# Graph-network kernel: 640 instead of 512 edges of a part taken from tables in SBUF, the logits of those edges turned on TensorE

## The chip, the cores and the metric

The kernel runs on one core of one Trainium2 chip. The core has five engines, each with its own in-order queue of instructions: PE (TensorE, matrix products; PEld is its weight load), DVE (VectorE), ACT (ScalarE), POOL (GpSimd, which here issues the indirect gathers) and SP (SyncE, which here only issues DMAs). The metric is device time in microseconds (us). Three runs of the kernel before gave 2940.52, 2941.33 and 2944.18 us, so the median is 2941.33 us.

## The reference

One layer of a graph network over 12,500 nodes with 128 features, and 412,500 edges that are sorted by destination (200,000 drawn edges in both directions, and a loop edge per node):

```python
theta = x[dst] - x[src]
w = sigmoid(relu(theta @ W1 + b1) @ W2 + b2)
agg = segment_sum(w * theta, dst, num_segments=n_nodes)
indeg = segment_sum(ones, dst, num_segments=n_nodes)
x = layernorm(x + agg + indeg * (x @ W4 + b4))
```

So each edge needs the row of its source, a hidden row of 128, one gate, and one weighted addition into its destination.

## The kernel before

A table z with `x @ W1` and x side by side (1 KB a node) is written to HBM first. Then the edges go by in parts. The first 18 parts ("plain") hold 1024 edges each, all of them gathered. The other edges go by in parts of `CE` = 1532. Of such a part up to 1024 edges are gathered: eight indirect DMAs on POOL (L401), each of 128 rows of z, into one of five buffers `zbuf`. The others, 512 slots, are "hot": their source is among the first 32 ranges of 256 nodes, and their rows come out of tables in SBUF (`tabs`, three bf16 terms a value) by a product with a one-hot matrix. There are 257 full hot parts and a rest of 344 edges, 258 parts in all. Two parts make a block of at most 104 destinations; a block's second part is a pass of the loop with h = 1, the first one with h = 0.

Which edge is hot is settled ahead by `place`, for 64 parts at a time: it walks the 32 ranges, and in each takes eight edges a list (a part is two lists of 766) by a MAX8 and a MATCH_REPLACE8 on DVE (L586, L589). Its steps are dealt out among the passes by a credit that each pass adds to (in `early_part` and `part`): 2.5 a pass in the hot parts before. The first such set is placed while the plain parts run, and the first hot gather needs its list of sources.

In a hot pass the engines are in an order written by hand (`manual_schedule`). PE takes, for the next part t: `hot_turned` (L1105, L1106: the hot rows' hidden values, 512 columns in the bank `pz`, first by the weights, then by the destination's row), `spread_y` (L893: the destinations' rows for the gathered edges), `hot_rows` (L1119: the logits of four groups of 128 hot edges, each a product whose moving operand is one column; L1122: the same edges' rows turned so that an edge lies on a partition), and then `issue`, which deals out the block's sums (L1158, with L1170, L1171 and L815 ahead of them where h = 1) and the 24 products of the hot tables (L1055, into the bank `pd`) in four runs. ACT takes, in this order, the relu (L1111), the sums' copy where h = 1 (L1213, L820), the hot rows' copy out of `pd` (L1069), the one-hots (L872, L873), the gates of the hot edges (L1128) and their weighing (L1131), the gates of the gathered edges (L975) and their weighing (L993), which frees the `zbuf` buffer. DVE subtracts, multiplies and adds up the gathered edges' hidden rows (L951, L956, L962), and makes the one-hots of the sums (L926, L1141), the hot tiles (L1039) and the normalization.

Of the kernel before, what the change touches and what calls it, by code (L numbers as in the profile page):

```python
# [36 lines left out]
NW = 3  # L37
AHEAD = 4
LB = 5
# [11 lines left out]
HK = HR * HS  # L51
HQ = HK // P
HOT = P * HT
LEADS = tuple(range(8))
OPENING = ((0,), (1, 7), (2, 6), (3, 5), (4,))
NU = 4
# [7 lines left out]
CE = 1532  # L64
# [5 lines left out]
HKL = HR * HE  # L70
# [14 lines left out]
def gnn_resnorm(  # L85
# [49 lines left out]
    assert HK == P * G and 2 * AW + D + WB <= 512 and LW <= SW  # L135
# [65 lines left out]
    of_buf = const.tile([P, max(HT * RG * HB * HS, BE)], F32, name="of")  # L201
    of_half = [of_buf.bitcast(BF16)[:, i * HT * RG * HB * HS:(i + 1) * HT * RG * HB * HS] for i in range(2)]
# [32 lines left out]
    wx_buf = [const.tile([P, K, AW], F32, name=f"wx{i}") for i in range(NW)]  # L235

    def table_load(c):
        n0, np_, m = chunks[c]
        xt = wx_buf[c % NW].rearrange("p k d -> p (k d)")[:, :BE]
        xt = xt.rearrange("p (t d) -> p t d", d=D)  # L240
        nc.scalar.dma_start(
            xt[:np_, :m, :], x[n0:n0 + np_ * m, :].rearrange("(p t) d -> p t d", t=m))
        return xt
# [11 lines left out]
    for name, v in (("w2_r", W2), ("b4_r", b4)):  # L255
        rows[name] = const.tile([P, D], F32, name=name)
# [13 lines left out]
    iota_row = const.tile([P, P], F32, name="iota_row")  # L270
# [36 lines left out]
    for i, t in enumerate(y2_buf):  # L307
        nc.vector.memset(t, 0.0)
        for h in range(SUB) if i < NY else (1,):
            nc.sync.dma_start(t[h * HALF + SW:h * HALF + SW + 1, :], b1.rearrange("(o d) -> o d", o=1))  # L310
# [43 lines left out]
    xT_all = const.tile([P, HX, HK], F32, name="xT")  # L354
    xT_flat = xT_all.rearrange("p j e -> p (j e)")
# [7 lines left out]
    assert late_at + 2 * NS <= HX * HK and WB + D <= 512  # L363
    hot_src = const.tile([P, NU, RG * HB * HS], F16, name="hot_src")
# [135 lines left out]
    def place(i, scratch, es, ed, bb, dp):  # L500
# [79 lines left out]
        tops = ep.tile([P, WL], F32, name="ed")[:, :HKL].rearrange("p (r e) -> p r e", e=HE)  # L580
        for r in range(HR):
# [3 lines left out]
            eight = tops[:, r, :]  # L585
            v.max(eight, left)  # L586
            v.tensor_scalar(eight, eight, FLOOR, None, op0=OP.max)
            yield "k"
            v.match_replace(left, eight, left, TAKEN)  # L589
            yield "k"  # L590
# [19 lines left out]
        yield "p"  # L610
        hrel = pp.tile([P, S2, HQ], BF16, name="hrel")
        pt = scratch()[:, :HQ * P].rearrange("p (q j) -> p q j", q=HQ)
        for q in range(HQ):
            nc.tensor.matmul(pt[:, q, :], hd[:, q * P:(q + 1) * P], ident_b, start=True, stop=True)
        yield "c"
        for q in range(HQ):
            for h in range(LISTS):
                a, e = max(h * HKL - q * P, 0), min((h + 1) * HKL - q * P, P)
                if a < e:
                    nc.scalar.activation(hrel[a:e, :, q], pt[a:e, q, h * S2:(h + 1) * S2], AF.Copy)  # L620
        hot_s = dram.tile([HR // RG, S2, LISTS, RG * HE], F16, name=f"hot_s{i}")
        rows_d = dram.tile([S2, RW], BF16, name=f"off_d{i}")
        for h, at in enumerate(lists):
            nc.sync.dma_start(hot_s[:, :n, h, :].rearrange("g p e -> p g e"),
                              hi[at].rearrange("p (g e) -> p g e", e=RG * HE))
            nc.sync.dma_start(
                rows_d[:n, BP:].rearrange("p (l m) -> p l m", l=LISTS)[:, h, :], far[at])
        hots[s0] = hot_s, hrel, n
        yield "s"
# [89 lines left out]
    with tc.manual_schedule(engines={SP}), tc.tile_pool(name="work", bufs=2) as wp, tc.tile_pool(  # L719
# [65 lines left out]
        def load_block(b):  # L785
            base = nc.values_load(base_b[0:1, b:b + 1], engines=[SP], min_val=0, max_val=N - WB,
                                  skip_runtime_bounds_check_because="base_b is at most N - WB")
            xw = wp.tile([P, D], F32, name="xw", bufs=5)
# [4 lines left out]
            if PLAIN <= b * SUB < PLAIN + NY * SUB:  # L793
                nc.vector.memset(y2[HALF:], 0.0)
            x2 = blocks[b]["x2"] = y2 if b >= W0 else x2_buf[b]
            for h in range(SUB):
# [5 lines left out]
                nc.sync.dma_start(to[h * HALF:h * HALF + SW, :], rows)  # L802
            if b * SUB >= PLAIN:
# [3 lines left out]
                for h in range(SUB):  # L807
                    nc.sync.dma_start(
                        to_all[h * HALF:(h + 1) * HALF, :],
                        rows_d[i + h:i + h + 1, :].to_broadcast([HALF, RW]))  # L810
# [71 lines left out]
        def spread_y(s):  # L882
# [3 lines left out]
            for k0 in range(0, K if s < PLAIN else J, J):  # L886
# [4 lines left out]
                d["y"].append(y)  # L891
                for j in range(J if s < PLAIN else pairs(s)):
                    nc.tensor.matmul(y[:, j, :], d["oh"][:, (k0 + j) * P:(k0 + j + 1) * P],  # L893
                                     y_of(s), start=True, stop=True)
# [73 lines left out]
        def lgh():  # L968

            return halves[1][:, :SUB * HQ].rearrange("p (i q) -> p i q", q=HQ)  # L970
# [10 lines left out]
        def weigh(s):  # L981
# [3 lines left out]
            for k in range(K):  # L985
                weighed[0] = nc.scalar.activation(wx[:, k, :D], zs[:, k, :] if s < NH else zs[:, k, D:],
                                                  AF.Copy, scale=wx[:, k, D:D + 1])

        def weigh_rest(s):

            wx = wx_of(s)
            for k in slots(s):
                weighed[0] = nc.scalar.activation(wx[:, k, :D], rows_of(s)[:, k, D:], AF.Copy,  # L993
                                                  scale=wx[:, k, D:D + 1])
# [7 lines left out]
        weighed = [None]  # L1002
# [9 lines left out]
        EP = RG * HS  # L1012
# [20 lines left out]
        def hot_tiles(f, x=0):  # L1033

            i0, g, i1, i = f
            w = (i1 - i0) * HS * RG
            of = hot_of(turn_of[0] % 2, x, w)
# [4 lines left out]
        def hot_products(f, x, pd, steps_of):  # L1042

            i0, g, i1, i = f
            w = (i1 - i0) * EP
            of = hot_of(turn_of[0] % 2, x, w)
            of = of.rearrange("p t (m r e) -> p t r m e", r=RG, e=HE)
            if not x:
                pd = ps_l.tile([P, G, P], F32, name="pd").rearrange("p g e -> p (g e)")
            bank, pd = pd, pd[:, x:x + w]  # L1050
            to = pd.rearrange("p (m r e) -> p r m e", r=RG, e=HE)
# [707 lines left out]
```

## Time and profile before

| | |
|---|---|
| median of three runs | 2941.33 us |
| the profiled execution, and its span from the first to the last instruction | 2943.8 us, 2942.0 us |
| busy share of the span: PE, PEld, DVE, ACT, POOL | 87%, 68%, 81%, 72%, 74% |
| mean granted TensorE clock | 0.937 |
| hot gathers (L401), issued from 269.3 to 2914.5 us | 2060, 980 ns each |

A row of the profile with an "x" says how many instructions it groups. A product of f32 operands stands as two records (two passes over the moving columns), so "x8" in a row of f32 products means four products. In a timeline the starts are what is added up here: a product's own duration reaches past the start of the next one.

### The profile page before, as it was taken

To read this page: it belongs to the slowest core of one execution; us is meant where nothing else is said; L and a number is where in the kernel's file an instruction comes from. 1 tells how busy PE (TensorE), PEld (TensorE's weight loads), DVE (VectorE), ACT (ScalarE), POOL (GpSimd) and SP (SyncE) were. 2 spreads that over 40 slices of the span, in tenths; PEclk is the share of its full clock that TensorE was granted. 3 is DMA by queue.
4 is the path that set the end of the run, shared out by engine and by line. 5 is a ranking of instruction groups with operands and counts; after the bars stand their busy time and mean duration, and the time that the engine had idled before them with its cause. 6 is when DMAs were issued, how large, how long until landed. Compare 5 with 4: busy or idle time off the path is not lost.

```text
span 2942.0 us, 59129 instructions
## 1 busy us (share of the span) xinstructions
PE 2548.2 (87%) x18606; PEld 2012.3 (68%) x18606; DVE 2380.3 (81%) x4436; ACT 2123.8 (72%) x6416; POOL 2164.5 (74%) x2213
## 2 busy tenths in 40 slices
PE   6877899988888998998898888898998888888886
PEld 5656677777676777776776666676776666677764
DVE  7899699888957988888558888888568888888654
ACT  6365778767777777677777777776777777677776
POOL 4566777777777777777777777777777777777774
PEclk8688999989999999999999999999999999999998
DMA  8455555555554555554554545454554555555542
GB/s 285 151 153 123 142 139 138 140 135 137 140 146 134 137 140 140 133 141 135 143 150 133 135 133 141 132 141 134 143 142 128 140 132 141 133 138 141 141 134 77
DMA packets 239329, 413.58 MB, mean 141 GB/s; under 512 B 63423, under 2 KB 147226, under 8 KB 237470
## 3 DMA queue, kind: packets, MB, share of 16 engines
q0 software_dynamic: 105280, 286.93, 35.3%
q1 hardware_dynamic: 131756, 116.40, 15.3%
q10 hardware_dynamic: 1970, 6.40, 0.7%
q8 instruction: 148, 2.42, 0.3%
q14 instruction: 175, 1.43, 0.2%
HBM read 388.57 MB, written 20.94 MB: 139 GB/s over the span
## 4 chain that ended last, share of the span: by engine, by line
PE 38%; ACT 19%; DVE 15%; DMA 11%; issue 7%; POOL 1%; DVEq 0%; SPq 0%; ACTq 0%; POOLq 0%
PE pa L1158 14%; DMA zbuf<-z,src_i 10%; DVE zbuf L951 5%; PE y L893 5%; PE pd L1055 5%; ACT wx L993 5%; PE px L1119 4%; ACT wxh L1131 4%; PE pz L1105 3%; PE pz L1106 3%; PE pz L1122 3%; ACT oh L872 2%; ACT oh L873 2%; ACT xT L1069 1%; ACT a L1213 1%
## 5 line engine op out<-in xcount | busy, mean ns | idle before, releaser
L401 POOL DMA_INDIRECT zbuf<-z,src_i x2060 | 2018.5, 980 | 637.0 <-issue 236.6
L993 ACT ACTIVATE wx<-zbuf,wx 128x128 f32<-128x128 f32 x2060 | 630.2, 388 | 0.0
L1158 PE MATMUL pa<-wx,ow 128*104 128x260 f32 (+1 forms) x2284 | 628.4, 393 | 0.0
L893 PEld LDWEIGHTS y<-y,oh 128*128 128x128 f32 (+1 forms) x2156 | 276.1, 197 | 420.5 <-DVE zbuf L951 378.2
L1055 PEld LDWEIGHTS <-tabs 128*128 128x128 bf16 x6360 | 452.8, 101 | 124.2 <-issue 8.2
L951 DVE TENSOR_TENSOR zbuf<-y,zbuf 128x1024 f32<-128x1024 f32 x258 | 315.1, 1221 | 272.2 <-DMA zbuf<-z,src_i 270.9
L1055 PE MATMUL pd<-of,tabs 128*128 128x128 bf16 (+3 forms) x6360 | 535.2, 223 | 0.0
L1111 ACT ACTIVATE hr<-pz 128x512 f32<-128x512 f32 x258 | 152.9, 593 | 522.9 <-PE pz L1106 522.8
L893 PE MATMUL y<-y,oh 128*128 128x128 f32 (+1 forms) x2156 | 314.7, 291 | 228.7 <-DVE zbuf L951 220.6
L1158 PEld LDWEIGHTS pa<-wx,ow 128*104 128x104 f32 x2284 | 342.8, 179 | 40.6 <-issue 0.4
L962 DVE TENSOR_REDUCE lg<-zbuf 128x8 f32<-128x1024 f32 x273 | 329.8, 1208 | 13.2
L956 DVE SCALAR_TENSOR_TENSOR zbuf<-zbuf,fix 128x1024 f32<-128x1024 f32 x273 | 331.6, 1215 | 9.3
L1158 PE MATMUL pa<-wxh,owh 128*104 128x130 f32 x2064 | 329.0, 296 | 0.0
L1131 ACT ACTIVATE wxh<-pz,wxh 128x128 f32<-128x128 f32 x1032 | 295.2, 369 | 42.1 <-PE pz L1122 35.9
L1105 PE MATMUL pz<-xT,wni 128*128 128x512 f32 x516 | 278.5, 621 | 1.6 <-ACT wxh L1131 1.6
L1158 PEld LDWEIGHTS pa<-wxh,owh 128*104 128x104 f32 x2064 | 274.3, 186 | 0.0
L1119 PEld LDWEIGHTS px<-w_c,hr 128*128 128x128 f32 x2064 | 263.5, 200 | 7.8 <-ACT hr L1111 7.8
L1119 PE MATMUL px<-w_c,hr 128*128 128x1 f32 x2064 | 262.1, 248 | 5.6 <-ACT hr L1111 5.6
L1106 PE MATMUL pz<-oh,y 128*128 128x512 f32 x516 | 264.5, 594 | 0.1
L872 ACT ACTIVATE oh<-to_all,away,mine 128x512 f32<-128x512 bf16 (+1 forms) x257 | 213.6, 831 | 3.1 <-DMA to_all<-off_d 3.1
L1106 PEld LDWEIGHTS pz<-oh,y 128*128 128x128 f32 x516 | 98.2, 191 | 124.3 <-issue 123.4
L1122 PE MATMUL pz<-wni,xT 128*128 128x128 f32 x1032 | 176.3, 297 | 0.0
(304 smaller groups left out, 3595.8 us busy)
## 6 DMA issues: line engine op xcount, KB each, us to landing
to_all<-off_d SPq DMA_DIRECT2D x258, 128.0 KB
zbuf<-z,src_i POOLq DMA_INDIRECT x2060
hot_src<-hot_s SPq DMA_DIRECT2D x228, 128.0 KB
y<-z SPq DMA_DIRECT2D x270, 28.0 KB
xw<-in_x_dram SPq DMA_DIRECT2D x138, 52.0 KB
out_dram<-o SPq DMA_DIRECT2D x138, 52.0 KB
wx<-in_x_dram ACTq DMA_DIRECT2D x12, 512.0 KB
z<-zbuf SPq DMA_DIRECT2D x6, 1024.0 KB
```

Of the source, the lines that this page charges most:

```text
L401: ins = nc.gpsimd.indirect_dma_start(out=rows_of(s)[:, k, :], out_offset=None, in_=z if s >= NH else x, in_offset=IndirectOffsetOnAxis(ap= ...
L893: nc.tensor.matmul(y[:, j, :], d["oh"][:, (k0 + j) * P:(k0 + j + 1) * P], y_of(s), start=True, stop=True)
L951: nc.vector.tensor_sub(half, yy.to_broadcast([P, 2, n, D]), half)
L956: nc.vector.scalar_tensor_tensor(h[:, at, :], h[:, at, :], 0.0, w2.to_broadcast([P, n, D]), op0=OP.max, op1=OP.mult)
L962: nc.vector.tensor_reduce(lg[:, at, 0], h[:, at, :], AX.X, OP.add)
L993: weighed[0] = nc.scalar.activation(wx[:, k, :D], rows_of(s)[:, k, D:], AF.Copy, scale=wx[:, k, D:D + 1])
L1055: steps_of.append(lambda q=q, i=i, t=t, j=j: nc.tensor.matmul(to[:, q], tabs[:, g, i, q, t, :], of[:, t, q], start=j == 0, stop=j == HT * ...
L1105: nc.tensor.matmul(pz, wneg, xT, start=True, stop=False)
L1106: nc.tensor.matmul(pz, y_of(t), blocks[t // SUB]["oh"][:, BP:], start=False, stop=True)
L1119: nc.tensor.matmul(lgh()[:, t % SUB, q:q + 1], hr[:, at], w2_c, start=True, stop=True)
L1131: nc.scalar.activation(wx[:, q, :D], pz[:, q * P:(q + 1) * P], AF.Copy, scale=wx[:, q, D:D + 1])
L1158: return [lambda i=i, one=one, w=w: nc.tensor.matmul(to if len(w.shape) == 3 else to[:, 0, :], one, w, start=first and i == 0, stop=last a ...
```

## The change

A part has 1608 edges of which 640 slots are hot: in each group of four ranges the first one gives 16 edges a list, the other three give 8 (`RU` = 5 units for `RG` = 4 ranges). That makes 245 full hot parts and a rest of 108 edges, 246 parts in place of 258, and four sets for `place` in place of five. What is done for 640 hot edges no longer fits one bank of 512: `hot_turned` and the relu are split in two lists of 320 (`pz` and `halves[1]`), the destination's rows of the two lists are taken from two halves of the partitions (64 each), `hot_rows` makes the logits as rows (five products with 32 equal columns of `W2`, each for 128 edges), the sigmoid runs on these rows (`hot_gates`), and PE turns the gates so that an edge is on a partition (`hot_gates_turned`), ahead of the sums and products. `hot_out` comes behind the gates. The products of the tables stay 24 for a part, six of them with 256 columns in place of 128. Loads differ too: each destination row goes to both halves, and `to_all` comes in four DMAs a block in place of two. The credit is 2.8 a pass and 6.5 in a plain part (5.5 before). Some buffers have fewer copies.

```diff
-NW = 3
+NW = 2
-LB = 5
+LB = 4
+RU = RG + 1
+HK = HR // RG * RU * HS
+ST = 32
-NU = 4
+NU = 3
-CE = 1532
+CE = 1608
...
         for r in range(HR):
...
-            eight = tops[:, r, :]
-            v.max(eight, left)
-            v.tensor_scalar(eight, eight, FLOOR, None, op0=OP.max)
-            yield "k"
-            v.match_replace(left, eight, left, TAKEN)
-            yield "k"
+            for _ in range(1 if r % RG else 2):
+                eight = tops[:, u, :]
+                u += 1
+                v.max(eight, left)
+                v.tensor_scalar(eight, eight, FLOOR, None, op0=OP.max)
+                yield "k"
+                v.match_replace(left, eight, left, TAKEN)
+                yield "k"
...
+                oh, rows = d["oh"], y_of(s)
+                if s >= PLAIN:
+                    at = slice(s % SUB * HALF, (s % SUB + 1) * HALF)
+                    oh, rows = oh[at], rows[at]
...
         def hot_turned(t):
...
-            nc.tensor.matmul(pz, wneg, xT, start=True, stop=False)
-            nc.tensor.matmul(pz, y_of(t), blocks[t // SUB]["oh"][:, BP:], start=False, stop=True)
+            oh = blocks[t // SUB]["oh"][:, BP + t % SUB * HKL:][:, :HKL]
+            banks = pz[:, :HKL], halves[1][:, :HKL]
+            for l, to in enumerate(banks):
+                nc.tensor.matmul(to, wneg, xT[:, l * HKL:(l + 1) * HKL], start=True, stop=False)
+            for l, to in enumerate(banks):
+                at = slice(l * HALF, (l + 1) * HALF)
+                nc.tensor.matmul(to, y_of(t)[at], oh[at], start=False, stop=True)
...
-            nc.scalar.activation(hr, pz, AF.Relu)
+            for l, bank in enumerate((pz, halves[1])):
+                nc.scalar.activation(hr[:, l * HKL:(l + 1) * HKL], bank[:, :HKL], AF.Relu)
...
-                nc.tensor.matmul(lgh()[:, t % SUB, q:q + 1], hr[:, at], w2_c, start=True, stop=True)
+                nc.tensor.matmul(rowed(q), w2_c.to_broadcast([P, ST]), hr[:, at], start=True, stop=True)
...
+        def hot_gates(t):
+
+            nc.scalar.activation(parts[t]["hr"][:, :2 * P], pz[:, 2 * P:], AF.Sigmoid, bias=b2_c)
+
+        def hot_gates_turned(t):
+
+            gates = parts[t]["hr"]
+            nc.tensor.transpose(pz[:, 2 * P:3 * P], gates[:, :P], ident)
+            for q in range(G, HQ):
+                at = slice((q - G) * ST, (q - G + 1) * ST)
+                newest[0] = nc.tensor.transpose(pz[:, 2 * P + q * ST:2 * P + (q + 1) * ST],
+                                                gates[at, P:2 * P], ident[at, at])
...
-            credit[0] = min(credit[0] + 2.5, 5.0)
+            credit[0] = min(credit[0] + 2.8, 5.0)
...
             if t < NS:
                 hot_rows(t)
+            if t < NS:
+                hot_gates(t)
+                hot_gates_turned(t)
+            while opened:
+                hot_out(*opened.pop(0))
+            last_out()
...
-                if h == 0:
+                if h == 1:
                     one_hot_h(b)
```

Two places of the order of instructions show it. On PE, in a pass with h = 0, from the start of `hot_turned` to the first products of the tables. Before (`px` is the bank of the logits, `pa` that of the sums, `owh` and `wxh` the hot edges' one-hots and weighed rows):

```order
L1105 MATMUL pz<-xT,wni 128x512
L1106 MATMUL pz<-oh,y_148 128x512
L893 MATMUL y<-y_146,oh 128x128 x4
L1119 MATMUL px<-w_c,hr 128x1 x4
L1122 MATMUL pz<-wni,xT 128x128 x4
L1158 MATMUL pa<-a,sh 104x130
L1158 MATMUL pa<-wxh,owh 104x130 x2
L1055 LDWEIGHTS tabs
L1055 MATMUL pd<-of,tabs 128x16x8
```

After (here `px` is the second bank, `halves[1]`; L1135 and L1138 are `hot_turned`, L910 `spread_y`, L1152 and L1155 `hot_rows`, L1164 and L1167 the gates' turn, L1203 the sums, L1081 the tables' products):

```order
L1135 MATMUL pz<-xT,wni 128x320
L1135 MATMUL px<-xT,wni 128x320
L1138 MATMUL pz<-oh,y_147 128x320
L1138 MATMUL px<-oh,y_147 128x320
L910 MATMUL y<-y_142,oh 128x128 x4
L1152 MATMUL pz<-hr,w_c 32x128 x5
L1155 MATMUL pz<-wni,xT 128x128 x2
L1155 MATMUL px<-wni,xT 128x128 x3
L1164 MATMUL pz<-wni,hr 128x128
L1167 MATMUL pz<-wni,hr 128x32
L1203 MATMUL pa<-a,sh 104x130
L1203 MATMUL pa<-wxh,owh 104x130 x2
```

Two products of 512 columns became four of 320, the products of one column became five of 128 columns on 32 output partitions, and two turns stand ahead of the sums. On ACT, in the same kind of pass, from the relu to the weighing of the hot edges, before:

```order
L1111 ACTIVATE hr<-pz 128x512
L1069 ACTIVATE xT<-pd 128x14x32
L1069 ACTIVATE xT<-pd 128x2x32
L872 ACTIVATE oh<-to_all,away,mine 128x512
L873 ACTIVATE oh<-oh 128x512
L1128 ACTIVATE wxh<-px,b_c 128x4
L1131 ACTIVATE wxh<-pz,wxh 128x128 x4
```

After:

```order
L1144 ACTIVATE hr<-pz 128x320
L1144 ACTIVATE hr<-px 128x320
L1159 ACTIVATE hr<-pz,b_c 128x256
L1096 ACTIVATE xT<-pd 128x14x32
L1096 ACTIVATE xT<-pd 128x2x32
L1096 ACTIVATE xT<-px 128x14x8
L1096 ACTIVATE xT<-px 128x2x8
L885 ACTIVATE oh<-to_all,away,mine 128x640
L886 ACTIVATE oh<-oh 128x640
L1174 ACTIVATE wxh<-pz 128x5
L1177 ACTIVATE wxh<-pz,wxh 128x128 x2
L1177 ACTIVATE wxh<-px,wxh 128x128 x3
```

The sigmoid (L1159) moved up to right behind the relu, so ACT now waits there for PE's logits, and five activations more stand in the pass.

186 lines of the change are left out of this document (107 added, 79 removed).

## The prediction

> **What bounds the kernel now.** I read the waits first, then the row of the gathers, then one long stretch by windows, and only then PE's timeline.
>
> ```profile
> POOL zbuf L401 <- issue: 260.0, 853, 0.3
> ACT hr L1111 <- PE pz L1106: 522.8, 196, 5.6
> PEld y L893 <- DVE zbuf L951: 378.2, 197, 9.7
> DVE zbuf L951 <- DMA zbuf<-z,src_i: 270.9, 138, 6.5
> ```
>
> ```profile
> L401 POOL DMA_INDIRECT zbuf<-z,src_i x2060: 942/949/1957, 269.3 to 2914.5; - x188
> ```
>
> ```profile
> 300.00:2700.00 2400.00, 2125.04 (x15778) 1675.80 (x15778) 1981.79 (x3591) 1783.97 (x5501) 1831.45 (x1866) 0.95 0.51 138
> ```
>
> ACT waits for PE, PE for DVE, DVE for the gathers' data, and POOL for nothing: its longest wait ahead of a hot gather is 0.3 us, the gap that always stands between two of them. From 269.3 to 2914.5 us it issues 2060 gathers, one in 1.2847 us. So the busiest engine by share, PE with 87%, is not the bound; the gathers' pace on POOL is. A block of two parts (16 gathers) takes 20.5 us, and 129 such pairs fill the 2645 us. The 269 us ahead and 27 us behind the last gather are opening and end.
>
> How much room PE has under that pace stands in a pair in which it did not wait:
>
> ```profile
> 1518.08 1.08 PE L1105 MATMUL pz<-xT,wni 128*128 128x512 f32 x2
> 1518.99 1.02 PE L1106 MATMUL pz<-oh,y 128*128 128x512 f32 x2
> 1519.85 1.05 PE L893 MATMUL y<-y,oh 128*128 128x128 f32 x8
> 1520.74 1.01 PE L1119 MATMUL px<-w_c,hr 128*128 128x1 f32 x8
> 1521.61 0.63 PE L1122 MATMUL pz<-wni,xT 128*128 128x128 f32 x4
> 1522.09 0.39 PE L1158 MATMUL pa<-a,sh 104*104 104x130 f32 x2
> ...
> 1522.76 0.50 PE L1055 MATMUL pd<-of,tabs 128*128 128x128 bf16 x6
> 1523.09 0.87 PE L1158 MATMUL pa<-wxh,owh 128*104 128x130 f32 x6
> 1523.79 0.50 PE L1055 MATMUL pd<-of,tabs 128*128 128x128 bf16 x6
> ...
> 1527.29 1.08 PE L1105 MATMUL pz<-xT,wni 128*128 128x512 f32 x2
> ...
> 1534.97 0.65 PE L1105 MATMUL pz<-xT,wni 128*128 128x512 f32 x1
> ```
>
> The part with the hot sums takes 9.21 us, the other 7.68, together 16.9: PE has 3.6 us of room in 20.5.
>
> **The change, part by part.** *Fewer gathers.* 245 full parts of eight and a rest of two make 1962, so 98 gathers go: 98 x 1.2847 = 126 us off POOL's time. That is the whole gain, and it holds only while a pair still takes 20.5 us. In general the hot stretch becomes 123 pairs in place of 129.
>
> *The opening.* The first hot gather waits for the first set of `place`, on DVE:
>
> ```profile
> L586 DVE MAX8 ed<-ew 128x8 f32<-128x767 f32 x32 | 30.6, 958 | 1.2 <-PE px L762 0.3
> L589 DVE MATCH_REPLACE8 ew<-ed,ew 128x767 f32<-128x767 f32 x32 | 30.1, 942 | 0.0
> L583 DVE TENSOR_SCALAR ew<-ew 128x767 int32<-128x767 int32 x31 | 17.7, 571 | 3.0 <-issue 2.1
> L587 DVE TENSOR_SCALAR ed<-ed 128x8 f32<-128x8 f32 x32 | 5.7, 179 | 0.9
> ```
>
> ```profile
> 100.00:260.00 160.00, 121.91 (x682) 93.21 (x682) 150.30 (x315) 90.07 (x212) 102.35 (x102) 0.79 0.50 135
> ```
>
> ```profile
> 269.25 0.95 POOL L401 DMA_INDIRECT zbuf<-z,src_i  x1 [9.26 <-ACT src_i L713]
> ```
>
> DVE is 94% busy from 100 to 260 us, so work added to it shows. Forty rounds in place of 32: 8 x (0.96 + 0.94 + 0.18) = 17 us, and 805 columns in place of 767 (5%) on the 78 us of the wide rows, 4 us, and some 3 us on the rest of the set. I take 24 us; the ends are 10 (the larger credit fills DVE's last idle) and 35. The sets that follow lie beside the hot passes, and there is one fewer; I cost them at nothing while DVE has room (1981.79 of 2400 us busy).
>
> *PE in a pair.* All prices come from starts in the rows above. An f32 product costs 0.91 us for 512 columns, so 1.78 ns a column. First what is certain, a part: five turns in place of four, +0.12 (0.48 for four); the gates' two turns, +0.18; six table products with 256 columns in place of 128, +0.33 (six take 0.33). In a pair, two more hot sums of 0.233, +0.47.
>
> *Half the array.* The destination's products use 64 partitions, the logits 32 output columns, the last gate's turn 32 partitions. The plain parts show what changing between half and whole costs:
>
> ```profile
> 130.12 0.48 PE L915 MATMUL y<-y,oh 64*128 64x128 f32 x2
> 130.54 0.49 PE L917 MATMUL y<-wni,xT 128*128 128x128 f32 x2
> 130.95 0.49 PE L915 MATMUL y<-y,oh 64*128 64x128 f32 x2
> ```
>
> There a product of 128 columns takes 0.42 us, against 0.22 for L893 above: 0.195 us at every change of shape. The new pass has five such changes (into the half products, to the logits, to the turns, to the last gate, to the sums): +0.98 a part. No row shows a change to 32 columns, so its ends are 0 and 0.195; I take the price of the nearest row, the 64 partitions.
>
> *Do the halves overlap?* `hot_turned` streams 640 columns by the weights (1.14 us) and 2 x 320 by the destinations. One after the other that is 2.28 us against 1.77: +0.51. If the two halves ran side by side it would be 1.71: -0.06. The five logit products cost 5 x 0.2225 = 1.11 against 0.87: +0.24; two at a time's price if the four column groups ran side by side, 0.45: -0.42. No row has two such products in neighbouring halves. So a pair costs 16.9 + 0.47 + 2 x (0.63 + 0.98 + 0.75) = 22.1 us without overlap and 16.9 + 0.47 + 2 x (0.63 + 0.98 - 0.48) = 19.6 with all of it. The rows are no nearer to one end than to the other, so I take the middle, 20.8.
>
> The Trainium skill (TensorEngine Tiling (Array Packing), Key Properties) says that different tiles run LDWEIGHTS and products in parallel, and TensorE: Matmul & The Clock Gate, Part 3, gives 3.07 times for four row tiles; no run here shows it. By that rule the pair would be at its lower end.
>
> *Waits.* PE and ACT now hand work to and fro once more: logits, sigmoid on ACT, turn on PE, with five turns of 0.6 us as the only cover for a sigmoid of about 0.4 us. If the relu is late behind ACT's weighing, everything behind it on PE waits. ACT itself has room:
>
> ```profile
> 1529.26 0.60 ACT L1111 ACTIVATE hr<-pz 128x512 f32<-128x512 f32 x1 [2.70 <-PE pz L1106]
> 1534.88 2.45 ACT L993 ACTIVATE wx<-zbuf,wx 128x128 f32<-128x128 f32 x8
> 1537.23 0.57 ACT L1111 ACTIVATE hr<-pz 128x512 f32<-128x512 f32 x1
> 1541.63 2.45 ACT L993 ACTIVATE wx<-zbuf,wx 128x128 f32<-128x128 f32 x8
> ```
>
> 8.0 us and 6.8 us, 14.8 a pair; the relu's second half, the sigmoid, a fifth weighing, the second copy and a wider one-hot add about 0.9 a part and 0.3 a pair: 16.9 of 20.5. What a pair waits when gathers don't hold it shows right after the opening:
>
> ```profile
> 306.88 1.12 PE L1105 MATMUL pz<-xT,wni 128*128 128x512 f32 x2 [0.36 <-ACT wxh L1131]
> 310.03 1.05 PE L1119 MATMUL px<-w_c,hr 128*128 128x1 f32 x8 [0.28 <-ACT hr L1111]
> 317.47 1.16 PE L893 MATMUL y<-y,oh 128*128 128x128 f32 x8 [0.52 <-DVE zbuf L951]
> 324.96 0.65 PE L1105 MATMUL pz<-xT,wni 128*128 128x512 f32 x1
> ```
>
> That pair took 18.1 us, 1.2 over the 16.9. So the waits lie between 0 and 1.2; I take 0.8, nearer the upper end because a link was added to the chain.
>
> *Loads.* SP issues two more row loads and two more pieces of `to_all` a block:
>
> ```profile
> 1499.69 0.35 SPq L802 DMA_DIRECT2D y<-z  x1
> ...
> 1500.13 1.09 SPq L808 DMA_DIRECT2D to_all<-off_d  x2
> ```
>
> That is 2 x 0.35 + 2 x 0.55 = 1.8 us of an engine that does nothing else, two blocks ahead of use: 0; uncovered it would be 1.8 a pair.
>
> *Sum.* A pair takes 20.8 + 0.8 = 21.6 us, more than POOL's 20.5, so PE becomes the bound: 123 x 21.6 = 2657 against 2645, +12, and +24 for the opening. 2942 + 36 = 2978 us of span. The profiled execution took 2943.8, 1.8 over its span and 2.5 over the median, so 2978 of span stands for about 2977 of median; I say 2975. Break-even lies at (2645 - 24) / 123 = 21.3 us a pair, 0.3 under my estimate.
>
> **The rivals.** *The gathers stay the bound.* If halves overlap in full, or the changes to 32 columns cost nothing (three of the five changes, 1.2 us a pair), PE needs 20.4 or less, waits included, and the pair stays at 20.5. Then 2942 + 24 - 126 = 2840. For it speak the 3.6 us of room; against it that five of them are claimed one by one above. It decides below 21.3, and is whole at 20.5.
>
> *No overlap at all.* 22.1 + 0.8 = 22.9: 123 x 22.9 = 2817, +172 and +24, so about 3135. For it speaks that every row of the trace has PE's products in single file.
>
> *The change doesn't do what it says.* If a part had more than 1024 edges that no hot slot takes, the general path behind the flag would run, for many times the time; with 32.9 edges a range on average (1608 x 256 / 12500) the slots fill nearly always, so I give it nothing.
>
> **How the numbers follow.** No change that could be told is +-0.2%, 2935 to 2947. PE the bound with part of the overlap: 0.37 slower (2947 to 3020, likeliest 2975), 0.05 within, 0.08 faster (2880 to 2935). Gathers the bound: 0.30, at 2840. No overlap: 0.20, 3040 to 3135. So faster 0.38, same 0.05, slower 0.57. The range reaches from the gathers' case, 2838, to 3080, and leaves out most of the last case above. The likeliest case alone has 2880 to 3020.
>
> **What would show it.** Right: gaps above 0.3 us ahead of the hot gathers, their releaser the weighing on ACT; ACT's wait for the relu and DVE's for gathered data gone; PE at 95% and its clock near full; a pair at 21 to 22 us; the first hot gather at 280 to 305 us. The overlap shows in the starts of the two L1138 products and the five of L1152, the changes of shape in the first product behind each. Wrong: gathers still 0.3 us apart throughout (rival one), or halves in single file (rival two).

## The result, and the profile after

The changed kernel takes 3652.42 us (median of 4 runs, 3646.04 to 3659.94), against 2940.93 for the kernel before in the same session: a ratio of 1.242, 95% interval 1.239 to 1.246. The forecast was 2975, in a range of 2838 to 3080. The direction was right; the loss is some twenty times the forecast one and lies far outside the range. The profiled execution has a span of 3644.1 us and a mean granted clock of 0.879 (before: 2942.0 and 0.937).

The row of the hot gathers on POOL, the kernel after:

```profile
L405 POOL DMA_INDIRECT zbuf<-z,src_i x1962: 940/947/1764, 306.2 to 3580.9; - x197
```

The first one comes at 306.2 us, 37 later than before. From there to the last are 3274.7 us for 1962 gathers, so 16 of them, a pair of parts, take 26.7 us. Before it was 20.5, and the forecast 21.6. Of the 702 us by which the span grew, 37 lie ahead of the first hot gather, 629 in this pace, and 36 behind the last one: from there to the end are 63.2 us in place of 27.5.

The list of waits, the kernel after (us in all, times, the longest):

```profile
POOL zbuf L405 <- ACT wx L1014: 918.9, 478, 19.3
DVE a L1269 <- ACT xuT L833: 813.7, 119, 15.6
ACT wxh L1177 <- PE px L1081: 756.8, 241, 6.7
...
PEld y L910 <- DVE zbuf L968: 303.1, 121, 10.7
ACT hr L1159 <- PE pz L1155: 266.3, 211, 5.4
```

In the list of before POOL's largest wait was the 0.3 us between two gathers. Now it waits 919 us for `zbuf` buffers, which the gathered edges' weighing on ACT (L1014, L993 before) frees. DVE's 271 us for the gathers' data have shrunk to 5. One row has no counterpart at all: ACT waits 757 us, 241 times, 3.1 us each, ahead of the hot edges' weighing (L1177, L1131 before), for the products of the hot tables (L1081, L1055 before). DVE's wait for ACT's copy of the sums (L1269 for L833) grew from 51.6 us to 814; what it costs by itself was not tested.

The same stretch as in the prediction's row, now for the kernel after (columns: PE, PEld, DVE, ACT and POOL busy, granted clock, share of the DMA engines, GB/s):

```profile
300.00:3500.00 3200.00, 2668.16 (x18604) 1940.16 (x18605) 1975.41 (x3429) 2079.35 (x6691) 1847.95 (x1912) 0.89 0.42 112
```

No engine is busy all the time: PE is busy 83%, ACT 65%, DVE 62%, POOL 58%. That fits a chain that goes round through several engines, each waiting for the next.

One turn of the chain is in the timeline of the kernel after, a pass with h = 0 (start, duration, then in brackets the wait ahead of it and its releaser):

```profile
1528.94 1.49 PE L1081 MATMUL pd<-of,tabs 128*128 128x256 bf16 x6
...
1529.15 0.63 ACT L1177 ACTIVATE wxh<-pz,wxh 128x128 f32<-128x128 f32 x2
...
1534.95 0.50 PE L1081 MATMUL px<-of,tabs 128*128 128x128 bf16 x6
1535.28 0.76 PE L1135 MATMUL pz<-xT,wni 128*128 128x320 f32 x2
1535.48 0.89 ACT L1177 ACTIVATE wxh<-px,wxh 128x128 f32<-128x128 f32 x3 [5.71 <-PE px L1081]
...
1536.42 0.81 PE L1135 MATMUL px<-xT,wni 128*128 128x320 f32 x2 [0.38 <-ACT wxh L1177]
...
1536.60 2.44 ACT L1014 ACTIVATE wx<-zbuf,wx 128x128 f32<-128x128 f32 x8
...
1537.16 0.53 PE L1138 MATMUL pz<-oh,y 64*128 64x320 f32 x1
1537.16 0.53 PE L1138 MATMUL px<-oh,y 64*128 64x320 f32 x1
1537.27 0.94 POOL L405 DMA_INDIRECT zbuf<-z,src_i  x1 [7.29 <-ACT wx L1014]
...
1537.53 0.43 PE L1138 MATMUL pz<-oh,y 64*128 64x320 f32 x1
1537.54 0.43 PE L1138 MATMUL px<-oh,y 64*128 64x320 f32 x1
...
1537.81 1.05 PE L910 MATMUL y<-y,oh 64*128 64x128 f32 x8
...
1538.95 0.41 ACT L1144 ACTIVATE hr<-pz 128x320 f32<-128x320 f32 x1
...
1539.41 0.74 PE L1152 MATMUL pz<-hr,w_c 128*32 128x128 f32 x10 [0.56 <-ACT hr L1144]
...
1542.47 0.82 PE L1081 MATMUL pd<-of,tabs 128*128 128x256 bf16 x6
```

ACT has weighed two of the five groups of hot edges by 1529.8. The other three were turned into the bank `px`, and PE finished that long ago. But the last of the four runs of the tables' products writes into the same bank, into its last quarter, and it stands at the end of PE's block. The program's wait is on the bank's tile and asks for the newest product in it, so ACT sits for 5.71 us, with nothing of its own data missing. Behind it in ACT's queue stand the gathered edges' gates and weighing (L1014), then the next relu (L1144). So POOL waits 7.29 us for its buffer, where 0.3 is usual, and PE waits for the relu. Each engine's delay comes back to it through the others.

The Trainium skill (PSUM — Partial Sum Buffer, the section on bank collisions) asks for semaphores by bank and partition quadrant, not by address, since two engines must not be on the same bank and quadrant at once. By that rule the wait could not simply be dropped, whatever columns are read. The trace agrees with it as far as it shows where the program waits: 241 waits, between columns 384 to 511 written and 0 to 383 read.

Two lines of the code say it, the first in `hot_products` and the second the bank that `turned_at` returns for the groups 2 to 4:

```
last = halves[1][:, 3 * P:3 * P + HB * EB] if halves else wide()[:, :HB * EB]
return (pz, halves[1])[q // 2 if q < 2 else 1][:, (q if q < 2 else q - 2) * P:][:, :P]
```

The waits also cost clock. PE's granted clock is the third column from the end, here in short stretches of the kernel after:

```profile
1516.00:1522.00 6.00, 3.96 (x27) 2.21 (x26) 4.30 (x9) 4.79 (x18) 4.26 (x5) 1.00 0.40 114
1522.00:1528.00 6.00, 3.95 (x27) 2.69 (x26) 5.86 (x11) 4.80 (x9) 4.48 (x6) 0.69 0.60 154
1528.00:1531.00 3.00, 3.00 (x16) 2.62 (x15) 2.73 (x4) 1.71 (x5) 1.67 (x2) 0.50 0.78 208
```

PE idled 4.1 of the first 12 us, and by the end of them had half its clock: the six products with 256 columns took 1.49 us at 1528.94, against 0.82 at 1542.47.

### The profile page after: what moved, and what is told of

It is laid out like the page before. It is cut to its first block, busy times and chain, and to the rows that moved or that the text cites. A ratio compares the mean times of both kernels' runs of the same rounds, so it can differ in the third digit from the quotient of the medians.

```text
span 3644.1 us, 63969 instructions
## 1 busy us (share of the span) xinstructions
PE 2988.2 (82%) x20496; PEld 2188.3 (60%) x20496; DVE 2290.1 (63%) x4117; ACT 2319.1 (64%) x7325; POOL 2038.2 (56%) x2115
## 4 chain that ended last, share of the span: by engine, by line
PE 48%; ACT 27%; DVE 6%; DMA 5%; issue 4%; POOL 2%; SPq 0%; DVEq 0%; ACTq 0%; POOLq 0%
PE pa L1203 21%; ACT wx L1014 10%; PE pd L1081 8%; PE pz L1152 5%; ACT wxh L1177 4%; DMA zbuf<-z,src_i 4%; PE y L910 4%; DVE zbuf L968 3%; PE pz L1155 3%; ACT hr L1159 2%; POOL zbuf L405 2%; PE pz L1164 2%; PE px L1081 2%; ACT xT L1096 1%; ACT hr L1144 1%
## 5 line engine op out<-in xcount | busy, mean ns | idle before, releaser
L1177 ACT ACTIVATE wxh<-px,wxh 128x128 f32<-128x128 f32 x738 | 217.6, 366 | 756.8 <-PE px L1081 756.8
L1014 ACT ACTIVATE wx<-zbuf,wx 128x128 f32<-128x128 f32 x1962 | 600.0, 388 | 0.0
L1203 PE MATMUL pa<-wx,ow 128*104 128x260 f32 (+1 forms) x2186 | 587.8, 388 | 0.0
L1081 PEld LDWEIGHTS <-tabs 128*128 128x128 bf16 x6072 | 488.9, 103 | 143.0 <-issue 0.8
L1269 DVE TENSOR_TENSOR a<-a,pa 104x130 f32<-104x130 f32 x123 | 35.8, 291 | 815.5 <-ACT xuT L833 813.7
L910 PE MATMUL y<-y,oh 64*128 64x128 f32 x2058 | 309.7, 296 | 253.9 <-DVE zbuf L968 241.1
L1081 PE MATMUL pd<-of,tabs 128*128 128x256 bf16 (+3 forms) x4554 | 504.4, 252 | 0.0
L910 PEld LDWEIGHTS y<-y,oh 64*128 64x128 f32 x2058 | 280.8, 203 | 340.8 <-DVE zbuf L968 303.1
L1203 PE MATMUL pa<-wxh,owh 128*104 128x130 f32 x2460 | 424.7, 322 | 0.0
L1203 PEld LDWEIGHTS pa<-wxh,owh 128*104 128x104 f32 x2460 | 381.0, 212 | 4.8
L1203 PEld LDWEIGHTS pa<-wx,ow 128*104 128x104 f32 x2186 | 328.6, 179 | 40.3 <-issue 0.7
L979 DVE TENSOR_REDUCE lg<-zbuf 128x8 f32<-128x1024 f32 (+1 forms) x261 | 314.9, 1207 | 12.9
L973 DVE SCALAR_TENSOR_TENSOR zbuf<-zbuf,fix 128x1024 f32<-128x1024 f32 (+1 forms) x261 | 316.6, 1213 | 8.9
L968 DVE TENSOR_TENSOR zbuf<-y,zbuf 128x1024 f32<-128x1024 f32 x246 | 299.4, 1217 | 5.4 <-DMA zbuf<-z,src_i 4.8
L1159 ACT ACTIVATE hr<-pz,b_c 128x256 f32<-128x256 f32 x246 | 116.7, 474 | 267.5 <-PE pz L1155 266.3
L1135 PE MATMUL px<-xT,wni 128*128 128x320 f32 x492 | 199.6, 488 | 88.4 <-ACT wxh L1177 88.2
L1152 PE MATMUL pz<-hr,w_c 128*32 128x128 f32 x2460 | 190.4, 311 | 86.2 <-ACT hr L1144 86.2
L885 ACT ACTIVATE oh<-to_all,away,mine 128x640 f32<-128x640 bf16 (+1 forms) x245 | 218.6, 892 | 19.4 <-DMA to_all<-off_d 19.4
L1135 PE MATMUL pz<-xT,wni 128*128 128x320 f32 x492 | 188.6, 465 | 19.2 <-ACT wxh L1177 19.2
L1138 PE MATMUL pz<-oh,y 64*128 64x320 f32 x492 | 200.5, 488 | 4.3 <-ACT oh L886 4.3
```

Source lines behind the costliest of these rows:

```text
L885: nc.scalar.activation(oh, blocks[b]["to_all"][:, c0:c1], AF.Abs, scale=mine, bias=away)
L910: nc.tensor.matmul(y[:, j, :], oh[:, (k0 + j) * P:(k0 + j + 1) * P], rows, start=True, stop=True)
L968: nc.vector.tensor_sub(half, yy.to_broadcast([P, 2, n, D]), half)
L973: nc.vector.scalar_tensor_tensor(h[:, at, :], h[:, at, :], 0.0, w2.to_broadcast([P, n, D]), op0=OP.max, op1=OP.mult)
L979: nc.vector.tensor_reduce(lg[:, at, 0], h[:, at, :], AX.X, OP.add)
L1081: steps_of.append(lambda to=to, i=i, q=q, t=t, j=j, a=of[:, t, :, e0:e1]: nc.tensor.matmul(to, tabs[:, g, i, q, t, :], a, start=j == 0, st ...
```

## The experiments

All of them are in the order in which they ran. Three kernels, the sixth to the eighth, compute the reference's values in another way; the third and fourth leave the square root out. The paces in the table are from the first to the last hot gather, for 16 gathers.

| kernel | time, us | ratio to before (95%) | first hot gather | 16 gathers |
|---|---|---|---|---|
| before | 2941 to 2944 | 1 | 269 | 20.5 |
| after | 3652.4 | 1.242 (1.239 to 1.246) | 306.2 | 26.7 |
| 1: after, weighing ahead of the products | 3203.6 | 1.087 (1.085 to 1.089) | 305.8 | 23.1 |
| 2: before, with the wait | 3137.0 | 1.065 (1.063 to 1.067) | 270.6 | 21.8 |
| 3: as 1, no table loads | 3089.1 | 1.050 (1.048 to 1.052) | 305.1 | 22.2 |
| 5: as 1, copies early | 3145.9 | 1.069 (1.068 to 1.071) | 308.6 | 22.7 |
| 6: 3 and 5 | 3074.2 | 1.045 (1.043 to 1.047) | 306.5 | 22.1 |
| 7: as 6, placing dealt out thinner | 3033.1 | 1.030 (1.029 to 1.032) | 307.5 | 21.8 |
| 8: as 7, older credit in the opening | 3039.1 | 1.033 (1.031 to 1.035) | 312.1 | 21.8 |

**1. The weighing of the hot edges ahead of the products.** No engine's order of instructions changes; only which of two instructions on one bank comes first in the program.

```diff
+            if h == 1 and b < NK:
+                shift(b)
+            if t < NS:
+                hot_weights(t)
             issue(sums, products_of_tiles())
-            if h == 1 and b < NK:
-                shift(b)
-            if t < NS:
-                hot_weights(t)
```

> The changed kernel, with the weighing of the part's hot edges (and the shift ahead of it) written ahead of the block of sums and table products. No engine's order of instructions changes; what changes is that ACT's third to fifth weighing copies no longer wait for the fourth run of the tables' products, which writes other columns of the same bank, and that this run waits for the copies. Theory 1 (the new wait of the weighing on the tables' products, 757 us in 241 waits, is what made the changed kernel slow): the waits of L1177's line on the products nearly vanish, the POOL gathers' 919 us of gaps shrink to under 250 us, a pair takes 20.5 to 22 us in place of 26.9, and the time is 2840 to 3030 us. Theory 2 (PE's own work is the bound: changes of shape, half products and a clock that falls): the waits move elsewhere, the pair stays above 25 us, and the time stays above 3400 us.

Measured: 3203.6 us, 449 less than the changed kernel. In the list of waits of this kernel the row of L1177 is gone, the last run of the tables' products waits for ACT only 23 us in all, and POOL's wait is halved:

```profile
POOL zbuf L405 <- ACT wx L1014: 485.4, 470, 25.7
...
DVE xw L1297 <- ACT xw L1279: 248.1, 83, 24.6
PEld y L910 <- DVE zbuf L968: 220.3, 120, 9.9
...
PE px L1081 <- ACT wxh L1177: 23.3, 5, 20.8
```

So the one wait, with what it sets off, is 449 of the 711 us: neither theory's number is met. The first gave 2840 to 3030, the second over 3400. The wait is shown as the largest cause, and it is not the only one.

This kernel shows what a pair costs PE. Its timeline has the starts of the gates' turns (L1164) and the only row of PE's products between them with a wait above 0.3 (L910); the starts of L1152 and L1155 show what the five logit products take:

```profile
2898.26 0.33 PE L1164 MATMUL pz<-wni,hr 128*128 128x128 f32 x1 [0.30 <-ACT hr L1159]
...
2906.05 1.16 PE L910 MATMUL y<-y,oh 64*128 64x128 f32 x8 [1.20 <-DVE zbuf L968]
...
2907.14 0.62 PE L1152 MATMUL pz<-hr,w_c 128*32 128x128 f32 x10
...
2907.69 0.44 PE L1155 MATMUL pz<-wni,xT 128*128 128x128 f32 x2
...
2908.75 0.33 PE L1164 MATMUL pz<-wni,hr 128*128 128x128 f32 x1 [0.30 <-ACT hr L1159]
...
2919.68 0.33 PE L1164 MATMUL pz<-wni,hr 128*128 128x128 f32 x1 [0.30 <-ACT hr L1159]
```

From 2898.26 to 2919.68 are 21.4 us, of which 1.8 are waits: PE's own work is 19.6 us a pair.

**2. The same wait put into the kernel before.** The third weighing copy of a pass waits for the pass's last product of the tables, which is a wait on PE that the kernel before does not have.

```diff
-                nc.scalar.activation(wx[:, q, :D], pz[:, q * P:(q + 1) * P], AF.Copy,
-                                     scale=wx[:, q, D:D + 1])
+                ins = nc.scalar.activation(wx[:, q, :D], pz[:, q * P:(q + 1) * P], AF.Copy,
+                                           scale=wx[:, q, D:D + 1])
+                if q == 2 and t > PLAIN:
+                    tc.add_manual_dep(ins.ins, newest[0].ins.name, ...)
```

> The kernel before, with one wait added: the third of the four hot weighing copies of a pass (L1131, ACT) waits for the pass's last product of the hot tables on PE, as the changed kernel's does. Nothing else changes. Theory 1: this wait alone gives most of the loss; ACT then comes to the gates and weighing of the gathered edges some 3 to 5 us later in each of 239 passes, POOL waits for its buffers, and the time goes from 2941 to 3200 to 3600 us (pairs of 22.5 to 26 us). Theory 2: the older kernel's 3.6 us of room a pair takes it up, and the time stays below 3050 us.

Measured: 3137.0 us, 193 more than before, a little under the first theory's range and well over the second's. The wait itself is as large as in the changed kernel:

```profile
ACT wxh L1131 <- PE pd L1055: 785.1, 254, 6.8
...
POOL zbuf L401 <- ACT wx L993: 312.7, 495, 13.1
```

785 us of waiting on ACT cost 193 of time here. By the starts of L1119 in its trace most pairs still take 20.6 us, next to 20.5 before: there the wait costs almost nothing. The 26 pairs with the square root's table loads (next experiment) take 24.4 on average, together 101 us above 20.5; most of the rest lies in the pairs in which a set of `place` begins (33 us), and behind the last gather (60.5 us in place of 27.5). In the changed kernel PE has 0.9 us of room (20.5 less 19.6) and makes up for little. The same wait has two prices; that the room of the engine behind it decides which is argued from these two kernels, which differ in more than the room.

**3 and 4. The function tables of ACT.** In the first experiment's kernel most pairs without placing took 20.9 to 21.1 us, and every fourth took 25.4: the pairs with a square root, once for `LB` = 4 blocks. Its timeline:

```profile
2770.06 1.28 ACT L1314 ACT_TABLE_LOAD   x1
...
2772.03 0.74 PE L1152 MATMUL pz<-hr,w_c 128*32 128x128 f32 x10 [0.78 <-ACT hr L1144]
...
2773.22 1.28 ACT L1159 ACT_TABLE_LOAD   x1 [0.92 <-PE pz L1155]
...
2775.05 0.47 PE L1164 MATMUL pz<-wni,hr 128*128 128x128 f32 x1 [1.45 <-ACT hr L1159]
...
2777.11 1.49 PE L1081 MATMUL pd<-of,tabs 128*128 128x256 bf16 x6
```

The square root's table goes in ahead of the relu, the sigmoid's ahead of the gates, on which PE's turn waits. PE loses 2.2 us to the two waits, and then part of the clock: the six products at 2777.11 take 1.49 us in place of 0.82. In experiment 3 (as 1) and 4 (as before) the square root is replaced by a relu, and the normalization is not the reference's:

```diff
-                nc.scalar.activation(sd[:WB, :m], mv[:WB, :m, 1], AF.Sqrt, bias=eps_c[:WB])
+                nc.scalar.activation(sd[:WB, :m], mv[:WB, :m, 1], AF.Relu, bias=eps_c[:WB])
```

> The kernel of the first experiment (hot edges weighed ahead of the products), whose square root on ACT (L1314, one in four blocks) is replaced by the relu of the same operand, which needs no load of a function table; the normalization is then not the reference's. There, pairs without a square root took 20.9 to 21.1 us, those with one 25.4, since the square root's table (1.28 us) and the sigmoid's (1.28 us) are loaded between PE's logits and PE's turn of the gates. Theory 1 (those loads now lie on PE's path): 30 pairs lose 4.3 us each, so 3204 falls to 3050 to 3110 us. Theory 2 (every fourth pair is long for another cause, such as the normalization's work on DVE): 3185 to 3210 us.

> The kernel before with the same replacement of the square root by a relu (the normalization is then not the reference's). 29 pairs of table loads of 2.57 us are 74 us of ACT. Theory 1: with the gathers as the bound they were hidden, so 2941 stays within 10 us. Theory 2: they cost time whatever the bound: 2870 to 2915 us.

The first run of 3, 4, 5 and 6 fell on a chip on which the kernel before takes 4142 us, and 3 took 4641, 4 took 4140, 5 took 4673 and 6 took 4629. On that chip another limit rules (last section), so these runs tell little: 4 against before is a ratio of 1.000 (0.995 to 1.006). That says nothing of the chips on which the gathers are the bound, and this control was not run there. 3 was run again:

> The third experiment's kernel once more, since on the chip of its first run the kernel before took 4142 us. The expectation for a chip on which the kernel before takes 2941 us stays: if the table loads lie on PE's path, 3050 to 3110 us against the 3204 of the first experiment; if every fourth pair is long for another cause, 3185 to 3210. On a slow chip neither can be told.

Measured: 3089.1 us, 115 less than experiment 1, and the fourth pair is 21.1 like the others. The first theory holds. What the same loads, in every fifth pair, cost the kernel before was not measured on such a chip, but its list of waits shows that they held up no hot gather:

```profile
POOL zbuf L401 <- ACT wx L993: 143.3, 470, 0.3
```

POOL's longest wait for a buffer that the weighing frees is 0.3 us, the usual gap.

**5. Two small copies earlier on ACT.** DVE's normalization waits for L1277 and L1279, and DVE's next subtraction (L968), for which PE waits, is behind it.

```diff
             last_out()
+            if done_b:
+                own(b - 1)
             if h == 0 and b + 1 < NK:
...
             if t < NS:
                 hot_weights(t)
-            if done_b:
-                own(b - 1)
```

> The kernel of the first experiment, with the two small copies on ACT that the normalization waits for (L1277, L1279) written ahead of the one-hots instead of behind the weighing of the hot edges. DVE then does not wait 3.9 us a pair for them, and its subtraction, on which PE's destination products (L910) wait 1.2 us in a pair of 21.1, comes earlier. Theory 1 (DVE's in-order wait makes PE late): the 248 us of DVE's wait fall under 60, the quiet pair goes from 21.1 to 20.3 to 20.7 us, and the time from 3204 to 3100 to 3170 us. Theory 2 (PE's own work fills the pair): 3190 to 3215 us.

> The fifth experiment's kernel once more, for the same reason. If DVE's in-order wait for the two small copies makes PE late, 3100 to 3170 us; if PE's own work fills the pair, 3190 to 3215.

Measured in the second run: 3145.9 us, 58 less than experiment 1. The pairs without placing and without a square root take 20.4 to 20.5 us. So 0.6 us of the 21.1 of a quiet pair were DVE's place in the order.

**6. Both, and the reference's values.** The reciprocal square root is made on DVE.

```diff
-                nc.vector.reciprocal(sd[:WB, :m], sd[:WB, :m])
+                nc.vector.tensor_scalar(r, mv[:WB, :m, 1], EPS, None, op0=OP.add)
+                nc.vector.tensor_scalar(y.bitcast(I32), r.bitcast(I32), 1, None, op0=OP.logical_shift_right)
+                nc.vector.tensor_scalar(y.bitcast(I32), y.bitcast(I32), -1, 0x5f3759df,
+                                        op0=OP.mult, op1=OP.add)
+                for _ in range(2):
+                    nc.vector.tensor_mul(q, y, y)
+                    nc.vector.scalar_tensor_tensor(q, q, -0.5, r, op0=OP.mult, op1=OP.mult)
+                    nc.vector.scalar_tensor_tensor(y, q, 1.5, y, op0=OP.add, op1=OP.mult)
...
-                nc.scalar.activation(sd[:WB, :m], mv[:WB, :m, 1], AF.Sqrt, bias=eps_c[:WB])
```

> The kernel of the fifth experiment (small copies early), with the reciprocal square root made on DVE by two integer instructions and two steps of Newton's iteration in place of ACT's square root and DVE's reciprocal, so without any load of a table in the hot parts. If both causes add up, 3204 loses 130 us and another 35 to 100: 2970 to 3080 us. If only one holds, 3050 to 3170.

> The sixth experiment's kernel once more. If both causes hold, 2970 to 3080 us; if one, 3050 to 3170.

Measured in the second run: 3074.2 us, 129 less than experiment 1, where 115 and 58 would give 172; the nine instructions on DVE lengthen the pairs in which DVE is full. A stretch of this kernel in which no set is placed, 2345 to 2755 us, shows what bounds a pair that nothing disturbs. First its window, then its waits:

```profile
2345.00:2755.00 410.00, 387.08 (x3133) 298.15 (x3126) 250.14 (x427) 329.71 (x1104) 306.52 (x321) 1.00 0.55 145
```

```profile
POOL zbuf L405 <- issue: 33.8, 111, 0.3
...
POOL zbuf L405 <- ACT wx L1014: 28.2, 79, 1.1
...
PE pz L1164 <- ACT hr L1159: 12.2, 40, 0.6
...
PE px L1081 <- ACT wxh L1177: 10.7, 20, 0.6
```

20 pairs in 410 us, 20.5 each, and a clock of 1.00. That is the pace of the kernel before, but it is not the gathers that set it. DVE never waits for a gather's data in this stretch (42.5 us in the same stretch of before), and POOL waits up to 1.1 us for a buffer. PE is busy 387.1 of the 410 us, and the other 22.9 are the two waits for ACT above. So a pair is PE's 19.4 us and 1.1 of hand-overs to ACT; that it comes to the same 20.5 is chance. Had all 123 pairs gone like this, the time would be 2942 + 37 - 126 = 2853 us.

**7 and 8. Placing and the opening.** In experiment 6 the pairs with placing take up to 28 us, and the pairs in which a set begins 33 us; ahead of the last set one takes 50. Kernel 7 gives the later sets a credit of 2.4 in place of 2.8 and ends the first step of `place` ahead of DVE's wait for ACT. Kernel 8 is kernel 7 with 5.5 in the plain parts.

```diff
+        yield "s"
         v.memset(left[:, HL:], 0.0)
...
-            credit[0] = min(credit[0] + 2.8, 5.0)
+            credit[0] = min(credit[0] + (2.8 if s < PLAIN + 56 else 2.4), 5.0)
```

```diff
-            credit[0] = min(credit[0] + 6.5, 6.5) if s < PLAIN - 5 else 200.0
+            credit[0] = min(credit[0] + 5.5, 5.5) if s < PLAIN - 5 else 200.0
```

> The sixth experiment's kernel, with the placing of the later sets dealt out more thinly (credit 2.4 a pass in place of 2.8 from the 57th hot part on; the first of these sets has too few passes for less) and with the first step of a set cut in two, so that DVE does not wait 6 us behind ACT's weighing. In the sixth experiment's run the pairs without placing took 20.5 us, those with it up to 28, and the three starts of a set 31 to 50. Theory 1 (what is left over 2942 is placing on DVE, which PE can no longer make up for): the starts lose some 6 us each and two of three sets some 10 to 25 us each, so 3074 goes to 3005 to 3040 us. Theory 2 (something else in the same stretch is the cause): 3065 to 3080.

> The seventh kernel, with the credit of the plain parts back at 5.5 (the value of the kernel before). In the changed kernel the first hot gather was issued at 306 us, against 269 before. If the larger credit crowds the opening's passes, it comes at 290 to 300 and the time falls 5 to 15 us against the seventh kernel; if the larger credit is what the longer placing needs, the rest of the set is placed in one go at the end of the plain parts, and the time rises by 5 to 20 us.

Their first runs (4624.0 and 4628.2 us, before 4142) and second runs (4725.4 and 4720.8, before 4052) fell on chips like that of the first run of 3, with the same expectation; they can't be told apart there. The third:

> The seventh kernel a third time; both runs so far fell on chips on which the kernel before takes over 4050 us and PE waits for its own instructions. On a chip where the kernel before takes 2941 us: if placing on DVE is what is left, 3005 to 3040 us; if not, 3065 to 3080.

> The eighth kernel a third time. If the larger credit crowds the opening, the first hot gather comes at 290 to 300 us and the time is 5 to 15 us below the seventh kernel's; if the longer placing needs it, 5 to 20 us above.

Measured: 3033.1 and 3039.1 us. Placing thinner gave 41 us, as the first theory said; 89 us over the kernel before are left. The older credit in the opening costs 6 us, and the first hot gather comes at 312.1 in place of 307.5: the longer placing needs the larger credit.

No version came out under the kernel before. What kernel 7 still has above the 2853 of an undisturbed run is some 180 us. By the starts of the gates' turns 131 of them are in the 89 pairs in which instructions of `place` run, and 24 behind the last gather (51.2 us in place of 27.5). The other 25 are one pair of 45.1 us, the one of 50 in experiment 6. In it ACT waits for a load of `to_all`, which stands in SP's queue behind the loads of the last set, one of them for 15 us:

```profile
ACT oh L886 <- DMA to_all<-off_d: 23.2, 1, 23.2
```

```profile
1681.46 15.10 SPq L191 DMA_DIRECT2D ed<-in_dst_dram  x1
```

The changed kernel has this wait too, 19.4 us; the kernel before has none. Nearly all other pairs without placing take 20.4 to 20.5 us in kernel 7. Why those loads stand so long in SP's queue, and why the time behind the last gather grew, was not tested.

## Why the prediction was wrong

**What bounds before** stood: POOL waits for no buffer there, and DVE waits for the gathers' data. **That PE becomes the bound** held where nothing disturbs a pair (experiment 6), at 20.5 us in place of 21.6. In the changed kernel as a whole PE is busy 83%, and its waits rule.

**Fewer gathers**: 1962, as said. The 126 us hold only at 20.5 us a pair, as the prediction put it; at 26.7 they turned into +629 (3274.7 against 2645.2).

**The opening** was put at +24 (10 to 35) and came to +37. The step's work was right. Up to the first hot gather DVE's busy time in these two windows (the kernel after, then before) grew by 25 us:

```profile
0.00:306.20 306.20, 208.86 (x1139) 167.86 (x1139) 259.41 (x589) 149.69 (x338) 142.92 (x153) 0.75 0.52 158
```

```profile
0.00:269.30 269.30, 200.40 (x1141) 159.39 (x1142) 234.12 (x557) 147.56 (x330) 146.07 (x154) 0.78 0.59 179
```

Its idle time grew as well, from 35.2 to 46.8 us, which the step had at nothing or as a gain. The end, which the sum took over from before at 27 us, grew by 36.

**PE in a pair, half the array, the overlap**: the sum between 19.6 and 22.1 was right at its lower end. PE's own 19.6 us are shown by experiment 1; the single terms, the changes of shape above all, were not measured one by one. The two halves run side by side: the two L1138 products of one pass over the columns start at 1537.16 together, the second pair at 1537.53 and 1537.54, and the next product at 1537.81, 0.65 us for both lists where one after the other would take 1.14. The Trainium skill's rule (TensorEngine Tiling (Array Packing), Key Properties, tiles operate independently) is borne out by this trace. The five logit products overlap as well: 0.55 us from the first (2907.14 in experiment 1) to the next line's start (2907.69), where one after the other would take 1.11. Taking the middle, 20.8, was 1.2 too much. That the forecast had the right direction rests on this error, so it is luck: with 19.6 and the 0.8 of waits a pair would have come out at 20.4, under the gathers' 20.5, and the forecast at 2840.

**Waits** is the step that failed: "between 0 and 1.2; I take 0.8". In place of 0.8 a pair has some 7 (26.7 less 19.6, with the loss of clock in it). In a pair that nothing disturbs the term was nearly right: 1.1 us in experiment 6. Four things were missing, in the order of their size as the runs show it:

- The wait of L1177 for L1081, 449 us. The prediction counted L1177's fifth copy as time on ACT and did not ask what its source bank waits for. The step "the products of the tables stay" was costed by PE's time alone, but their last run now goes to the bank of the hot edges' rows.
- The table loads, 115 us. They were in the profile of before, and the prediction put a sigmoid between two of PE's steps without asking which table ACT holds then. The text named the hand-over to ACT as a risk and priced it from a pair of before, in which no such load lay on the path.
- DVE's place in the order, 58 us: the copies for the normalization behind a longer weighing.
- Placing in the hot passes, costed at "nothing while DVE has room". DVE has room on average (62% busy), but not in the pairs with the most steps, nor where it waits for ACT at a set's start; 41 us of it are shown by experiment 7.

**Loads** were put at 0. Once in the run ACT waits 19.4 us for `to_all` (experiment 7), a small part of the loss.

**"ACT itself has room"** was right as a sum and no help. The estimate was 16.9 us a pair; 2079.35 us in a stretch of 3200 are 17.3 in 26.7. (The two stretches that it added up to 14.8 overlap, from 1534.88 to 1537.23; the row of the long stretch gives 15.2 a pair, 1783.97 of 2400 us times 20.5.) What counted was the order in its queue.

**The size of the room.** The bounds for the waits came from a pair of before with 3.6 us to spare. Experiment 2 shows what room does: 785 us of the same waiting cost 193 us there, and nothing in most pairs.

**The rivals.** "The gathers stay the bound" did not come even where nothing disturbs a pair: in that stretch of experiment 6 POOL waits for buffers, and DVE for no gather. "No overlap at all" is refuted by the starts of L1138. The case that came, a new wait through a shared bank, was none of them. Of the signs listed, POOL's gaps with the weighing on ACT as releaser and the vanished wait of DVE came true. PE at 95% and a clock near full did not, and that alone tells a chain of waits from an engine at its limit; both are there in the quiet stretch of experiment 6 (387.1 of 410 us, 1.00).

**Open.** Some buffers have fewer copies in the changed kernel, and no run puts them back. In quiet pairs they cost no more than the 1.1 us that PE waits; what they cost elsewhere, and what DVE's 814 us of waiting cost, is not known.

## What to carry to other kernels

When work moves to another buffer, list for each bank of PSUM who writes and who reads it and in which program order, and not only how long each engine works: in this program a read that comes behind an unrelated write to its bank waits for that write. Price a new hand-over between two engines by what else is in both queues at that moment, function tables among it, and take the bound from a place that has as little room as the new one. A change that uses up the slack of the engine that is not the bound lets other disturbances count that the slack had hidden.

## What the runs showed of the hardware that was not expected

On three of the six chips that the runs fell on, the kernel before takes 4052 to 4142 us in place of 2942. In the profile of experiment 4 on one of them, the mean granted clock is 0.81 in place of 0.94, and among PE's waits are many with no engine as releaser:

```profile
PEld L1055 <- issue: 545.7, 590, 2.7
...
PE pd L1055 <- issue: 448.6, 444, 2.6
```

Its timeline shows them on single products in the middle of PE's block, while a gather on POOL takes the same 0.946 us in the median as elsewhere (second fence):

```profile
2002.17 0.27 PE L1158 MATMUL pa<-wxh,owh 128*104 128x130 f32 x1 [1.08 <-issue]
2002.28 0.22 PE L1055 MATMUL pd<-of,tabs 128*128 128x128 bf16 x1
2004.29 0.27 PE L1055 MATMUL pd<-of,tabs 128*128 128x128 bf16 x1 [1.79 <-issue]
```

```profile
L401 POOL DMA_INDIRECT zbuf<-z,src_i x2060: 940/946/1897, 300.1 to 4088.7; - x188
```

What holds PE's instructions back there stays open. The changed kernel itself was not run on such a chip; its variants 3, 5, 6, 7 and 8 were 12 to 17% slower than before there.
